# ScalarE's copies of a projection put in front of tile 0's block, in the layers of 8 heads

## The chip, the cores and the metric

The kernel runs on one core of one Trainium2 chip. A core has TensorE (matrix products, PE in the profile), VectorE (DVE), ScalarE (ACT), GpSimd (POOL) and SyncE (SP, which here only starts DMA transfers). Each engine works through its own stream of instructions in order; engines wait for each other by semaphores. The metric is device time in microseconds (us), the median of several executions. All arithmetic of the layers is in float32.

## The reference

Two graph attention layers of 8 heads and one of a single head over 4096 nodes of 512 features. The adjacency matrix is dense int32, but only about 0.2% of it is ones, with more in the first rows and columns. The heart of each layer, cut to what matters:

```python
h = jnp.einsum('nf,kfp->knp', node_matrix, W)          # projection, 8 heads of 64
f1 = jnp.einsum('knp,kp->kn', h, a_src)
f2 = jnp.einsum('knp,kp->kn', h, a_dst)
e = jax.nn.leaky_relu(f2[:, :, None] + f1[:, None, :], negative_slope=ALPHA)
e = jnp.where(adjacency_matrix[None, :, :] > 0, e, NEG_INF)
att = jax.nn.softmax(e, axis=-1)
out = jnp.einsum('knm,kmp->knp', att, h)
...
x = _layernorm(x + _L0_gnn_ref(...))                   # layer 0
h = jax.nn.elu(_gat_heads(x, mask, W1, a1))            # layer 1, 8 heads
h2 = _gat_heads(x1, mask, Wo[None], ao[None])[0]       # layer 2, 1 head of 512
out = jax.nn.relu(elu(h2) @ lin1_w + lin1_b) @ lin2_w + lin2_b
return _layernorm(x + out)
```

## The kernel before

The nodes are cut into 32 tiles of 128. The kernel first finds the edges of tiles 1 to 31 and lists them, while it projects the input for layer 0 (0 to about 325 us of the profile). Then come the two layers of 8 heads (`heads_layer`, L1679: about 325 to 850 us, and 850 to 1305 us), and then the layer of one head with the two linear layers and the last norm.

A layer of 8 heads reads a table in DRAM with one row for each node: 8 heads of 64 projected features, each with the node's score. Tiles 1 to 31 gather the rows of their edges from that table (GpSimd's indirect DMA, L1350), in units of at most six chunks of 128 edges. A unit's steps are: scores and two exponentials (`at.weights`, VectorE and ScalarE, L1442 to L1456), scaling of the gathered rows (`at.scale`, VectorE, L1507 and L1526) and the sums (`at.sum`, TensorE, L1548). Tile 0 has so many edges that it is done densely, by the class `First`: all 32 blocks of 128 rows of the table are loaded by SyncE (`ask`, L1592), `make` turns a block's scores into weights on ScalarE (L1607 to L1612, 18 instructions), `sort_out` masks them on VectorE (L1620), and `add` sums two blocks at a time on TensorE (L1634).

When a tile is finished it goes straight on to the projection of the next layer, over a list of jobs called `ways`, each of which names the job that follows it:

- `divide`: division by the sum of weights and, in layer 0, the residual and the norm, in layer 1 the elu (VectorE, ScalarE L1656 and L1657, or L1667 and L1668)
- `norm`: the rest of that, then `turn_in`: four transposes on TensorE into `pt` (L714) and copies to `xt` on ScalarE (L717)
- `project`: eight matmuls on TensorE into two halves `ph` (L726)
- `rows`: `project_out`, ScalarE's copies of the halves to `hrow` (L753, and L749 where the next layer has one head) and of the scores to `ss_t` (L760), and the store of `hrow` to the next table by SyncE (L754)
- `row`, `split`: rows of tile 0's scores, and scores split into bfloat16 parts

`pt` and `ph` share two PSUM buffers (tag "ph", pool `ps`), so a transpose that follows a projection needs the copies of the projection's first half to be done. `xt` and `hrow` have two buffers each.

The loop of `heads_layer` has one step for each unit and is a manual schedule: each engine gets its instructions in the order of the Python text. In most of the layer the steps come in threes: a tile with few edges (one unit), then a tile with many (two units). The second step of the tile with many edges runs `project`, `make`, `rows` and the transposes of `norm`; the step after it runs `project`, `make`, `First.add` and `rows`; the third runs the transposes of `norm` only. The job list lets a job run one step after the job before it, save that `rows` follows `project` within the step.

Of the kernel before, what the change touches and what calls it, by code (L numbers as in the profile page):

```python
# [560 lines left out]
def sparse_path(  # L561
# [148 lines left out]
    def turn_in(sb, ps, st, src, t):  # L710

        pt = ps.tile([P, FC, P], F32, name="pt", tag="ph")
        for c in range(FC):
            nc.tensor.transpose(pt[:, c, :], src[:, ts(c, P)], ident)  # L714
        xt = sb.tile([P, FC, P], F32, name="xt")
        for c in range(FC):
            nc.scalar.activation(  # L717
                xt[:, c, :], pt[:, c, :], AF.Copy, accum_out=st.xparts[:, c, t : t + 1]
            )
        return xt  # L720
# [8 lines left out]
    def project_in(ps, st, columns, n=P):  # L729

        return [project_half(ps, st, columns, j, n) for j in range(2)]
# [46 lines left out]
    def row_of_s(diag, ps, st):  # L778

        per = min(st.heads, 4)  # L780
        for lo in range(0, st.heads, per):
            for h in range(per):
                nc.scalar.activation(diag[:, lo + h], ident, AF.Copy, scale=st.s[:, 0, lo + h : lo + h + 1])
            pr = ps.tile([P, 4, P], F32, name="pr", tag="ph")[:, :per]
            nc.tensor.matmul(pr, ones_w, diag[:, lo : lo + per], start=True, stop=True)
            nc.scalar.copy(st.s_row[:, lo : lo + per], pr)
# [525 lines left out]
    def units_of(order):  # L1312
        units = []
        for t in order:
            if t == 0:
                steps = math.ceil(NT / GC)
                cuts = [NT * i // steps for i in range(steps + 1)]
                units += [Whole(a, b) for a, b in zip(cuts, cuts[1:])]
                continue
            own = [  # L1320
                Unit(t, [(p.first + i, n) for i, n in runs], slots)
                for p in pts if p.t == t for runs, *slots in p.units()
            ]
            own[0].first = own[-1].last = True
            units += own
        return units
# [352 lines left out]
    def heads_layer(gp, wk, sb, pp, st, nxt, fetch, finish, clear):  # L1679

        many = [t for i in range(8) for t in (2 + i, NT // 2 - i)][: NT // 2 - 1]
        order = [t for pair in zip(range(NT - 1, NT // 2, -1), many) for t in pair] + [1]
        assert sorted(order) == list(range(1, NT))
        units = units_of(order)
        units[-1:] = units[-1].cut(units[-1].n - 2)
        units[:1] = units[0].cut(2)
        groups = [(1, 1), (2, 6), (8, 8), (16, 8), (24, 8)]  # L1690
        with tc.tile_pool(name=f"ha_{st.name}", bufs=2, space=PSUM, reuse_waits="tile") as pacc, \
                tc.tile_pool(name=f"hp_{st.name}", bufs=1, space=PSUM, reuse_waits="tile") as one, \
                tc.tile_pool(name=f"hq_{st.name}", bufs=2, space=PSUM, reuse_waits="tile") as ps, \
                tc.manual_schedule():
            at = Attention(st, gp, wk, pacc, one, whole)
            extra = {}
            if clear:
                for _ in range(GB):
                    nc.vector.memset(gp().rearrange("p k f -> p (k f)").bitcast(BF16), 0.0)
            first = First(at, whole, pacc, order[:-1] + [0, 1])  # L1700
            first.ask()
            for u in units[:GB]:
                at.gather(u)
            for t in order[:2]:
                extra[t] = fetch(t)
            for _ in range(DW):
                first.make()
                first.sort_out()
            first.add(DW)
            first.take()  # L1710
            for t in order[:2]:
                at.spread(t)()
            at.weights(units[0])

            def divide_first():
                at.inverse(sb, 0)
                o = at.normal(sb, 0, spare())
                finish(o, 0, extra.pop(0))()  # L1720
                return norm, 0, o, lambda: None

            def spare():
                return first.sb.tile([P, F + HS], F32, name="rows0", bufs=DW)[:, :F]

            def divide(t):
                at.inverse(sb, t)
                o = at.normal(sb, t)
                return norm, t, o, finish(o, t, extra.pop(t))

            def norm(t, o, rest):
                rest()
                xt = turn_in(pp, ps, nxt, o, t)
                return project, t, xt

            def project(t, xt):
                return rows, t, project_in(ps, nxt, lambda c: xt[:, c, :])

            def rows(t, halves):
                project_out(pp, nxt, halves, t)  # L1740
                out_.add(t)
                if t == 0:
                    return row, 0
                lo, n = next((lo, n) for lo, n in groups if lo <= t < lo + n)
                return (split, lo, n) if out_.issuperset(range(lo, lo + n)) else None

            def row(t):
                row_of_s(first.sb.tile([P, HS, P], F32, name="w0", bufs=DW), ps, nxt)

            def split(lo, n):  # L1750
                split_s(pp, nxt, lo, n)

            def run(of):

                mine = [way for way in ways if way[0] is of]
                for way in ([w for w in mine if w[1] != 0] or mine)[:1]:
                    ways.remove(way)
                    nxt_ = of(*way[1:])
                    if nxt_:
                        ways.append(nxt_)  # L1760

            ways, out_, resting = [], set(), None
            for i, u in enumerate(units):
                pos = order.index(u.t)
                spread = None
                if u.first and pos + 2 < NT - 1:
                    spread = at.spread(order[pos + 2])
                    extra[order[pos + 2]] = fetch(order[pos + 2])
                run(project)
                if i + 1 < len(units):  # L1770
                    at.weights(units[i + 1])
                taken = u.first and first.sorted - first.summed >= min(DB, NT - first.summed) > 0
                if i > 0:
                    first.make(i)
                held = None
                at.scale(u)
                first.take()
                if taken:
                    first.add(DB)
                    held = divide(order[pos - 1]) if pos > 0 else None  # L1780
                    if first.summed == NT:
                        extra[0] = fetch(0, spare())
                        resting = i + 2
                at.sum(u)
                if i + GB < len(units):
                    at.gather(units[i + GB])
                late_split = [way for way in ways if way[0] is split]
                run(rows)
                run(row)
                if first.sorted < first.made - 1 or first.made == NT:  # L1790
                    first.sort_out()
                run(norm)
                if held:
                    ways.append(held)
                elif u.first and pos > 0:
                    ways.append((divide, order[pos - 1]))
                    run(divide)
                if i == resting:
                    ways.append(divide_first())
                if spread:  # L1800
                    spread()
                if late_split:
                    run(split)
            assert resting and resting < len(units) - 4
            assert all(way[0] is split for way in ways)
            ways.append((divide, order[-1]))
            run(divide)
            mrow = mean_of_all_but(pp, ps, nxt, order[-1])
            while ways:
                for of in (project, rows, row, split, norm, divide):  # L1810
                    run(of)
                    if of is rows and len(out_) == NT:
                        finish_mean(ps, nxt, mrow)
# [99 lines left out]
    def gp():  # L1913

        turns[0] += 1
        return (keep if (turns[0] - 1) % GB < GT else more).tile([P, GC, F + HS], F32, name="g")
# [415 lines left out]
```

## Time and profile before

| what | value |
|---|---|
| median of 3 runs | 2067.4 us (2067.35 to 2068.75) |
| the profiled execution's own time | 2044.31 us |
| its span in the profile | 2042.5 us |
| PE / DVE / ACT / POOL busy over the span | 81% / 67% / 44% / 49% |
| PE, DVE, ACT busy in 325 to 850 us (layer 0) | 401.68, 400.91, 260.72 of 525.00 us |
| PE, DVE, ACT busy in 850 to 1305 us (layer 1) | 359.55, 307.34, 241.13 of 455.00 us |
| mean granted TensorE clock over the span | 0.912 of full speed |

In a line of the timeline stand the start, the duration, the engine, the line of the kernel, the operation and what it writes and reads, and in brackets how long the engine had stood idle before it and who ended that wait. "remote" or "another core or an unknown queue" means that the profile names no releaser; "issue" that it shows nothing that was waited for. In a list of waits the three numbers are the total, the number of times and the longest. A busy TensorE is not TensorE at its peak: the ends of matmuls are modelled.

### The profile page before, as it was taken

The page shows a single profiled execution, that of the slowest core. Times are in us where ns is not written, and L with a number is a line of the kernel's source. Part 1 is how long each engine was busy: PE and PEld are TensorE (multiplying, and loading weights), DVE is VectorE, ACT ScalarE, POOL GpSimd, SP SyncE. Part 2 cuts the span into 40 slices and gives each one's busy share as a digit, 9 for nine tenths or more (in the row PEclk, how much of TensorE's full clock was granted, in tenths as well). Part 3 has the DMA queues.
Part 4 walks back from the last instruction along what each step waited for, and adds up shares of the span by engine and source line. Part 5 has one row for each costly group of instructions (what it writes and reads, how often), then busy time and mean ns, then how long its engine had stood idle before and what let it go on. Part 6 is the DMA issues. An engine that isn't in the chain of part 4 may idle for free.

```text
span 2042.5 us, 31094 instructions
## 1 busy us (share of the span) xinstructions
PE 1660.7 (81%) x9797; PEld 1225.7 (60%) x9797; DVE 1360.8 (67%) x3539; ACT 905.5 (44%) x3292; POOL 1000.6 (49%) x1336
## 2 busy tenths in 40 slices
PE   4997975788788878588778787768899998989987
PEld 1675654466556655356556665446668776766776
DVE  6786764888877878377667675426665666656665
ACT  5986964555544636166556562212133221212211
POOL 5556565656654562566655455263432544435100
PEclk7998986888888999789999898878899999999998
DMA  8898855566666664556655555263345444445210
GB/s 309 293 340 285 310 198 165 174 196 195 196 187 188 190 202 132 158 162 175 179 152 150 145 154 166 92 210 112 92 150 164 137 127 125 117 126 139 63 42 33
DMA packets 140084, 343.69 MB, mean 168 GB/s; under 512 B 39525, under 2 KB 44653, under 8 KB 132230
## 3 DMA queue, kind: packets, MB, share of 16 engines
q0 software_dynamic: 64064, 180.85, 31.8%
q1 hardware_dynamic: 74246, 156.57, 22.1%
q10 hardware_dynamic: 1600, 4.19, 0.6%
q8 instruction: 80, 1.31, 0.3%
q14 instruction: 94, 0.77, 0.1%
HBM read 332.19 MB, written 42.24 MB: 183 GB/s over the span
## 4 chain that ended last, share of the span: by engine, by line
PE 46%; issue 12%; ACT 11%; DVE 11%; POOL 5%; another core or an unknown queue 3%; DMA 2%; ACTq 0%; POOLq 0%; DVEq 0%; SPq 0%
PE acc L1548 13%; PE ph L726 11%; PE acc L1634 5%; POOL g L1350 4%; ACT w L1610 3%; PE px L2059 3%; ACT rows L1612 2%; DMA g<-table_t,idx 2%; PE px L2067 2%; PE pt L714 2%; PE py L2059 2%; PE pz L2059 2%; ACT xt L717 1%; PE py L2067 1%
## 5 line engine op out<-in xcount | busy, mean ns | idle before, releaser
L1350 POOL DMA_INDIRECT g<-table_t,idx x774 | 816.3, 1055 | 733.1 <-PE acc L1548 317.6
L1548 PE MATMUL acc<-g,sm 128*64 128x260 f32 (+2 forms) x3408 | 474.8, 411 | 120.2 <-DVE sm L1515 53.1
L726 PE MATMUL ph<-sw_t,xt 128*128 128x264 f32 (+1 forms) x1536 | 408.4, 422 | 78.6 <-issue 35.6
L1548 PEld LDWEIGHTS acc<-g,sm 128*64 128x64 f32 x3408 | 270.7, 145 | 286.8 <-issue 79.6
L726 PEld LDWEIGHTS ph<-sw_t,xt 128*128 128x128 f32 x1536 | 313.4, 209 | 153.1 <-issue 42.4
L1526 DVE TENSOR_TENSOR g<-g,wp 128x2048 f32<-128x2048 f32 (+5 forms) x114 | 291.8, 2559 | 2.8 <-ACT wp L1456 2.8
L717 ACT ACTIVATE xt<-pt 128x128 f32<-128x128 f32 x256 | 67.3, 277 | 253.2 <-PE pt L714 207.2
L1610 ACT ACTIVATE w<-s_row,d 128x128 f32<-128x128 f32 x512 | 155.8, 386 | 0.0
L1634 PE MATMUL acc<-rows,w 128*128 128x65 f32 x1024 | 125.4, 283 | 18.9 <-DVE w L1620 18.7
L1634 PEld LDWEIGHTS acc<-rows,w 128*128 128x128 f32 x1024 | 125.3, 201 | 21.7 <-ACT rows L1608 19.2
L1158 DVE MAX8 cand<-key 128x8 f32<-128x85 f32 (+51 forms) x395 | 99.7, 316 | 45.0 <-PE key L992 44.9
L1612 ACT ACTIVATE rows<-rows 128x64 f32<-128x64 f32 x512 | 128.6, 334 | 0.0
L977 ACT ACTIVATE sg<-raw,value 128x2048 bf16<-128x2048 int32 x60 | 120.1, 2008 | 5.1 <-DMA raw<-in_adj_dram 4.7
L2073 ACT ACTIVATE shid<-shid,sl1b 128x256 f32<-128x256 f32 x112 | 50.5, 500 | 119.3 <-DVE shid L2011 111.6
L714 PE MATMUL pt<-s_ident,o 128*128 128x128 f32 x248 | 42.8, 298 | 56.9 <-ACT ss_t L760 34.6
L1667 ACT ACTIVATE rstd<-mv,s_eps 128x1 f32<-128x1 f32 x64 | 18.9, 295 | 140.7 <-DVE mv L1664 132.0
L1658 DVE SCALAR_TENSOR_TENSOR o<-ex,o 128x512 f32<-128x512 f32 x63 | 43.6, 691 | 53.2 <-ACT ex L1657 43.6
L1620 DVE SCALAR_TENSOR_TENSOR w<-w,mask 128x1024 f32<-128x1024 f32 x64 | 77.3, 1211 | 1.2 <-ACT w L1610 1.2
L714 PEld LDWEIGHTS pt<-s_ident,o 128*128 128x128 f32 x248 | 27.6, 146 | 83.0 <-ACT ss_t L760 40.1
L1555 DVE RECIPROCAL rd_t<-acc 128x8 f32<-128x8 f32 x62 | 12.7, 204 | 94.0 <-PE acc L1548 39.9
L1656 ACT ACTIVATE ex<-o 128x512 f32<-128x512 f32 x63 | 39.6, 629 | 77.2 <-DVE o L1574 55.0
L1515 DVE TENSOR_SCALAR sm<-iota_n,nl,w 128x64 f32<-128x64 f32 x284 | 68.4, 317 | 0.0
(283 smaller groups left out, 2839.6 us busy)
## 6 DMA issues: line engine op xcount, KB each, us to landing
raw<-in_adj_dram SPq DMA_DIRECT2D x60, 1024.0 KB
table_t<-hrow SPq DMA_DIRECT2D x64, 260.0 KB
rows<-table_t SPq DMA_DIRECT2D x64, 260.0 KB
xr<-in_x_dram SPq DMA_DIRECT2D x63, 256.0 KB
g<-table_t,idx POOLq DMA_INDIRECT x774
table_t<-hrow SPq DMA_DIRECT2D x32, 257.0 KB
xr<-sx_d SPq DMA_DIRECT2D x32, 256.0 KB
out_dram<-xr SPq DMA_DIRECT2D x32, 256.0 KB
```

Source lines behind the costliest of these rows:

```text
L714: nc.tensor.transpose(pt[:, c, :], src[:, ts(c, P)], ident)
L717: nc.scalar.activation(xt[:, c, :], pt[:, c, :], AF.Copy, accum_out=st.xparts[:, c, t : t + 1])
L726: nc.tensor.matmul(ph[:n], columns(c), st.w[:, c, j], start=(c == 0), stop=(c == FC - 1))
L977: nc.scalar.activation(sg[:, ts(i, w)], raw[:, ts(i, w)], AF.Sign, bias=values["half"])
L1158: nc.vector.max(out=cand[:, at : at + 8], in_=key[:, j - w0_ : j - w0_ + n_])
L1350: nc.gpsimd.indirect_dma_start(out=u.g[:, k, : self.st.row], out_offset=None, in_=self.st.table[:, :], in_offset=bass.IndirectOffsetOnAxis ...
L1526: nc.vector.tensor_mul(body, body, wp[:, :, None].to_broadcast(body.shape))
L1548: nc.tensor.matmul(out_[g * HN : (g + 1) * HN], sm[:, slot], rows(k), start=start, stop=stop)
L1610: nc.scalar.activation(w[:, h], self.st.s_row[:, h], AF.Exp, scale=0.8, bias=d8[:, h : h + 1])
L1612: nc.scalar.activation(rows[:, h, :DM], rows[:, h, :DM], AF.Copy, scale=rows[:, h, DM : DM + 1])
L1634: nc.tensor.matmul(acc[:, j, k * HD : (k + 1) * HD], w[:, h], rows[:, h * HD : (h + 1) * HD], start=(b == lo and k == 0), stop=(b == hi - ...
L2059: nc.tensor.matmul(out_[:, m], a[:, c, ts(k, P)], b[:, c], start=m == 0 and c == 0, stop=k == ks[-1] and c == 1,)
```

## The change

Two statements of the step move up: the list of `split` jobs that stood before this step's `rows`, and `run(rows)` itself. They stood behind `at.sum` and the gathers; now they stand in front of `first.make(i)`. No statement is added or removed.

```diff
@@ -1770,6 +1770,8 @@
                 if i + 1 < len(units):
                     at.weights(units[i + 1])
                 taken = u.first and first.sorted - first.summed >= min(DB, NT - first.summed) > 0
+                late_split = [way for way in ways if way[0] is split]
+                run(rows)
                 if i > 0:
                     first.make(i)
                 held = None
@@ -1784,8 +1786,6 @@
                 at.sum(u)
                 if i + GB < len(units):
                     at.gather(units[i + GB])
-                late_split = [way for way in ways if way[0] is split]
-                run(rows)
                 run(row)
                 if first.sorted < first.made - 1 or first.made == NT:
                     first.sort_out()
```

On ScalarE the copies L749, L753 and L760 of a step now stand ahead of the block L1607 to L1612 of the same step, and in layer 0 or 1 ahead of what `divide` issues within `held`. On SyncE the store L754 stands ahead of the loads L1592 and L1922 of the same step. The order on TensorE, VectorE and GpSimd is the same in both kernels.

## The prediction

> **What bounds the kernel now.** I read the page first, then the chain of waits through the two layers of 8 heads (325 to 1240 us), then the sum of waits there, then single steps in the timeline.
>
> From the page: the shares of the chain, and the groups concerned.
>
> ```profile
> PE 46%; issue 12%; ACT 11%; DVE 11%; POOL 5%; another core or an unknown queue 3%; DMA 2%; ACTq 0%; POOLq 0%; DVEq 0%; SPq 0%
> ...
> L1610 ACT ACTIVATE w<-s_row,d 128x128 f32<-128x128 f32 x512 | 155.8, 386 | 0.0
> ...
> L1612 ACT ACTIVATE rows<-rows 128x64 f32<-128x64 f32 x512 | 128.6, 334 | 0.0
> ```
>
> TensorE is the largest link, but ScalarE has 11%, and of it L1610 and L1612, the block of tile 0 that `make` issues, are the largest lines. The waits of 325 to 1240 us (total us, times, longest):
>
> ```profile
> ACT xt L717 <- remote: 39.5, 9, 8.0
> ...
> PE pt L714 <- ACT ss_t L760: 34.6, 12, 4.5
> ...
> ACT hrow L753 <- remote: 15.6, 9, 2.5
> ```
>
> TensorE's transposes wait for the small copies of L760 that `rows` makes. With the L753 and L749 waits of the same kind that is 54.7 us before L714 in this stretch. The timeline shows one such step of layer 1:
>
> ```profile
> 923.24 3.74 PE L726 MATMUL ph<-sw_t,xt 128*128 128x257 f32 x16 [0.76 <-issue]
> ...
> 925.35 0.16 ACT L1607 ACTIVATE d<-rows 128x8 f32<-128x8 f32 x1
> ...
> 926.90 1.97 PE L1548 MATMUL acc<-g,sm 128*64 128x260 f32 x16
> ...
> 928.00 2.00 ACT L1612 ACTIVATE rows<-rows 128x64 f32<-128x64 f32 x8
> ...
> 930.52 0.16 ACT L760 COPY ss_t<-ph 128x1 f32<-128x1 f32 x1
> ...
> 930.68 0.66 PE L714 MATMUL pt<-s_ident,o 128*128 128x128 f32 x4 [1.80 <-ACT ss_t L760]
> ...
> 931.37 0.28 ACT L717 ACTIVATE xt<-pt 128x128 f32<-128x128 f32 x1 [0.69 <-issue]
> ```
>
> The projection ends at 926.98, yet its copies start after the block, so the transposes stand 1.80 us. The round goes ScalarE's xt copies, projection, block, copies, transposes, xt copies. Of every three steps one has this round (call it the tight step): it projects, makes a block and transposes. The step before it makes no block, and the one after it transposes nothing. I count 11 tight steps in layer 0 and 11 in layer 1. Elsewhere ScalarE waits 4 to 10 us for the transposes and has room.
>
> **What the Trainium skill says.** "Perfetto Trace Analysis", section "Per-instruction lifecycle": ScalarE and VectorE are strict first in, first out. The trace agrees: the copies above, ready at 926.98, wait behind the block until 929.99. The same section: a matmul's end is computed, its semaphore comes later. The trace agrees strongly; at 1122.26 the sums of a tile end by the record, and who needs them starts at 1129.20:
>
> ```profile
> 1124.07 0.66 PE L714 MATMUL pt<-s_ident,o 128*128 128x128 f32 x4 [1.80 <-ACT hrow L749]
> ...
> 1129.20 0.21 DVE L1555 RECIPROCAL rd_t<-acc 128x8 f32<-128x8 f32 x1 [4.75 <-remote]
> ...
> 1132.04 0.28 ACT L717 ACTIVATE xt<-pt 128x128 f32<-128x128 f32 x1 [7.97 <-remote]
> ```
>
> "TensorE: Matmul & The Clock Gate", section "Part 1: The HAM clock gate": an idle window of about 3.4 us halves the clock. Here the granted clock falls to 0.50 in 1128 to 1132, and the projection after the tight step takes 5.2 to 6.6 us instead of 3.74 in some 17 of 22 cases.
>
> **The change, part by part.** It removes and adds no instruction. VectorE's, TensorE's and GpSimd's orders stay. On ScalarE the 4 or 5 copies of `rows` go in front of the 18 instructions of the block. On SyncE 15 table stores go ahead of the loads of tile 0's rows (L1592). POOL's queue is not passed.
>
> *The tight step.* Let P be the start of its projection and E the time at which ScalarE is done with the exponentials. Now: block 4.69 us (925.35 to 930.00 and alike), copies 0.74, transposes and hand-over 0.69; xt starts at E + 6.12. After: the copies must wait for the projection. What that gives is seen in a step that makes no block, at 774.20:
>
> ```profile
> 774.20 3.83 PE L726 MATMUL ph<-sw_t,xt 128*128 128x264 f32 x16 [0.46 <-issue]
> ...
> 778.07 0.38 ACT L753 COPY hrow<-ph 128x260 f32<-128x260 f32 x1 [1.40 <-PE ph L726]
> 778.34 0.23 ACT L760 COPY ss_t<-ph 128x4 f32<-128x4 f32 x2
> ```
>
> The second copy starts at P + 3.87, all are done at P + 4.43 (in layer 1, with one small copy less, P + 4.25). Then the block, then xt at once, for the transposes now lie beside the block. So xt starts at 4.69 after the later of E + 0.74 and P + 4.43. The block stays in the round: only the transposes leave it, and the wait for the projection enters.
> - Layer 0: E is P + 3.6 on average (2.4 to 4.8; L1456 writes the one `wp` buffer and stands up to 3.5 us before it). Over the 11 steps the differences are -0.69 to +0.57 us, sum -4.3 us.
> - Layer 1: E is P + 2.1. Before P + 8.13, after P + 8.94: +0.8 us in ten steps, 0 in one (E = P + 2.9). Sum +8.1 us.
> - Together +4 us. The 54.7 us before L714 are thus hardly to be had: the same ScalarE time is waited for by L717's reader, the next projection, instead.
>
> *Late hand-overs.* In the 22 steps xt starts later than E + 6.12 by 45.5 us in all, which the page mostly puts to a remote releaser: in order 1.3, 0, 0.6, 0.3, 3.8, 2.3, 3.4, 0.6, 4.7, 0, 0.5 in layer 0 and 3.2, 0, 2.6, 0, 5.2, 2.6, 3.8, 1.7, 7.3, 0, 1.8 in layer 1. After, transposes end near P + 6.4 to 7.3, about 2.2 us before the block ends; taking 2.2 us from each of the 22 excesses leaves 16.8, so 28.7 us gone. Against that the project-to-copy hand-over, now in front of the block, comes into the round. In the 14 steps without a block it was late by 0, 0.85, 2.2, 2.8, 4.0 or 4.7 us, 14.5 in all, 1.04 each; 22 times that is +22.8. Bounds: 0, if it is prompt while TensorE is busy behind it; and above, seven tight steps in which the second copy waited to P + 9 or later even behind the block, where the block would now start only then: 3.8 us each, +27 net. I take the mean, because the steps without a block have just the order that comes. Sum so far: +4 - 28.7 + 22.8 = -2 us.
>
> *The clock.* The stake is about 1.9 us in 17 projections, 32 us. TensorE's gap before the transposes (3.1 us in layer 0, 1.8 in layer 1, then a second one) becomes one gap behind them, shorter by the little that the round gains. Three of 17 back at full clock would be -6 us. Bounds 0 and -15; I take -6.
>
> *The step after it* (projection, block, no transposes): the copies wait for P + 3.9, at half clock P + 6.5, and the block, the layer norm's or elu's instructions and the next exponentials move back by 3 to 5.5 us. Behind them stands the xt copy that idles 4 to 10 us for the transposes: cost 0; without that cover 1 to 2 us in each of the few steps with only 4 us.
>
> *VectorE* waits up to 1.4 us longer for the block at L1620 in that step (930.79 above); behind it stand the next unit's scores and the scaling, needed only after the projection and tile 0's 3.5 us: 0. *SyncE*: a store waits for copies that end before tile 0's sums, for which the loads behind it wait anyway: 0; a late load would be felt only two steps on (REST).
>
> Sum -8 us of the profiled execution's 2044.31 us (span 2042.5). The median shown is 2067.4, 23 us more, so late hand-overs may be commoner there; I carry the difference: 2059.
>
> **The rivals.**
> - *Hand-overs and clock recover.* They come mostly where TensorE stands, and it now has its transposes early. All 45.5 us gone: -41.5 with the +4; 2026. For it: hand-overs behind a busy TensorE are mostly prompt (0 in 8 of 14). Against: TensorE still idles 2.4 us before the projection.
> - *The projection in front of the block*, the slower one. Place: the second copy of `rows` in the tight step. Price: all that it is late beyond E now delays 4.69 us of block and with it xt; decides once the copy is late by more than about 2 us per step on average. With the seven late steps as above and layer 1's +0.8: about +19; 2086. For it: 15.6 us of L753 waits even behind the block. Against: 774.20.
> - *Nothing changes*: the terms cancel within 0.2% (about what a measurement of this kernel tells from no change); 2067.
>
> **How the numbers follow.** Small gain 0.42 (own range 2045 to 2064), recovery 0.12, slower 0.32 (2072 to 2095), nothing 0.14. Faster 0.53, with nearly all of the first case; same 0.15; slower 0.32. The range 2034 to 2088 leaves out most of the recovery and the upper end of the slower case.
>
> **What would show it.** L714's waits for L760, L753 and L749 fall from 54.7 us to under 15. L753's waits for the projection rise from 18 us to over 60. L717 in the tight step starts right behind L1612, without idle, at P + 9. The idle before L726 grows. Wrong, if xt in the tight steps of layer 1 starts before P + 8.5, or if VectorE or PE waits for w at L1620 by more than 20 us, or if L753 in the tight steps waits past P + 6 in more than a third.

## The result, and the profile after

The changed kernel takes 2102.1 us (median of 6 runs, 2088.0 to 2106.4), the kernel before 2066.5 us beside it. The ratio of the runs is 1.0159 (95%: 1.0131 to 1.0186; the medians alone give 1.0172): 1.6% slower, where 0.4% faster had been predicted. The profiled execution took 2087.99 us (span 2086.3), 43.7 us more than that of before.

From the page of the changed kernel: the shares of the chain, and two of the costliest groups.

```profile
PE 47%; issue 11%; DVE 11%; ACT 11%; another core or an unknown queue 5%; POOL 4%; DMA 3%; POOLq 0%; DVEq 0%; ACTq 0%; SPq 0%
...
L726 PE MATMUL ph<-sw_t,xt 128*128 128x264 f32 (+1 forms) x1536 | 423.5, 434 | 126.2 <-ACT xt L717 61.6
...
L753 ACT COPY hrow<-ph 128x260 f32<-128x260 f32 (+2 forms) x128 | 47.8, 374 | 219.5 <-PE ph L726 146.6
```

Over the whole program ScalarE now idles 219.5 us ahead of the copies of L753. The share of the chain that has no releaser in the record rose from 3% to 5%. The waits of 325 to 1280 us (total us, times, longest):

```profile
ACT hrow L753 <- PE ph L726: 132.3, 71, 4.6
ACT xt L717 <- PE pt L714: 109.8, 30, 6.8
PE ph L726 <- ACT xt L717: 60.2, 34, 7.9
ACT hrow L753 <- remote: 57.5, 18, 5.9
...
DVE o L1658 <- ACT ex L1657: 22.7, 12, 2.4
...
DVE rstd L1672 <- ACT rstd L1668: 18.1, 12, 4.3
...
PE pt L714 <- ACT ss_t L760: 10.9, 4, 4.5
```

Two waits of the kernel before (325 to 1240 us) that belong beside these:

```profile
PE ph L726 <- ACT xt L717: 33.5, 23, 7.6
...
ACT hrow L753 <- PE ph L726: 18.2, 14, 2.4
```

The wait that the change was to remove is mostly gone: L714 waits for `rows`' copies 10.9 us instead of 54.7. In its place ScalarE waits in front of L753 for the projection, 132.3 and 57.5 us where it was 18.2 and 15.6, and the projection waits more for xt (60.2, before 33.5). VectorE's waits at L1658 and L1672 are new: in the kernel before they are 0 and 3.4 us.

One tight step of layer 0 in the timeline (start, us, engine, line; idle before it and its releaser in brackets):

```profile
402.65 3.83 PE L726 MATMUL ph<-sw_t,xt 128*128 128x264 f32 x16 [0.46 <-ACT xt L717]
...
406.75 1.97 PE L1548 MATMUL acc<-g,sm 128*64 128x260 f32 x16 [0.28 <-issue]
407.04 0.38 ACT L753 COPY hrow<-ph 128x260 f32<-128x260 f32 x1
412.76 0.38 ACT L753 COPY hrow<-ph 128x260 f32<-128x260 f32 x1 [5.34 <-remote]
...
413.25 0.68 PE L714 MATMUL pt<-s_ident,o 128*128 128x128 f32 x4 [4.52 <-ACT ss_t L760]
...
415.86 2.00 ACT L1612 ACTIVATE rows<-rows 128x64 f32<-128x64 f32 x8
417.77 0.25 ACT L717 ACTIVATE xt<-pt 128x128 f32<-128x128 f32 x1
...
418.17 1.25 PE L726 MATMUL ph<-sw_t,xt 128*128 128x264 f32 x2 [4.00 <-issue]
```

By the record the projection is done at 406.48, yet its second copy starts at 412.76, P + 10.1. The block follows it, xt follows the block at once, and the next projection starts after 4 us of idle, at half speed (6.69 us for all of it at a granted clock of 0.50, where the one before took 3.83 at 1.00). This is the picture of the slower rival.

I cut both traces at the first xt copy of every transposing step. The last xt copy of layer 1 comes 46 us later than before. Of these, the 22 tight steps have 14.8 us (252.0 to 266.8), the 22 steps after them 7.8 (358.9 to 366.7), the four intervals around the last blocks of the two layers 7.9 (56.8 to 64.7), the start of layer 1 5.5 (55.4 to 60.9), everything else about 10. Not all of this is the change's doing. The profiled execution of before was a quick one (2044 us, where the median is 2067), and a second profile of before (before_again, below) has 61.5 us at the start of layer 1 and 61.1 around the last blocks. A second profile of the changed kernel was taken on the same chip as that one, both near their medians. Between these two the last xt copy comes 24.2 us later: 16.9 from the tight steps (252.5 to 269.4), 4.6 from the steps after them (361.6 to 366.2), 2.6 from around the last blocks, and the rest about nothing. So the tight steps carry most of the loss.

### The profile page after: what moved, and what is told of

Read it like the earlier page. It is cut to its first block, busy times and chain, and to the rows that moved or that the text cites. A ratio compares the mean times of both kernels' runs of the same rounds, so it can differ in the third digit from the quotient of the medians.

```text
span 2086.3 us, 31062 instructions
## 1 busy us (share of the span) xinstructions
PE 1669.0 (80%) x9777; PEld 1232.9 (59%) x9797; DVE 1363.4 (65%) x3539; ACT 912.4 (44%) x3292; POOL 999.0 (48%) x1336
## 4 chain that ended last, share of the span: by engine, by line
PE 47%; issue 11%; DVE 11%; ACT 11%; another core or an unknown queue 5%; POOL 4%; DMA 3%; POOLq 0%; DVEq 0%; ACTq 0%; SPq 0%
PE ph L726 15%; PE acc L1548 13%; PE acc L1634 4%; ACT w L1610 3%; POOL g L1350 3%; PE px L2059 3%; ACT rows L1612 2%; PE py L2059 2%; DMA g<-table_t,idx 2%; PE px L2067 2%; PE pz L2059 2%; DVE g L1526 1%; DVE xr L2011 1%; PE acc L1478 1%
## 5 line engine op out<-in xcount | busy, mean ns | idle before, releaser
L726 PE MATMUL ph<-sw_t,xt 128*128 128x264 f32 (+1 forms) x1536 | 423.5, 434 | 126.2 <-ACT xt L717 61.6
L726 PEld LDWEIGHTS ph<-sw_t,xt 128*128 128x128 f32 x1536 | 323.6, 216 | 206.5 <-ACT xt L717 68.8
L1610 ACT ACTIVATE w<-s_row,d 128x128 f32<-128x128 f32 x512 | 155.8, 386 | 0.0
L753 ACT COPY hrow<-ph 128x260 f32<-128x260 f32 (+2 forms) x128 | 47.8, 374 | 219.5 <-PE ph L726 146.6
L717 ACT ACTIVATE xt<-pt 128x128 f32<-128x128 f32 x256 | 66.6, 272 | 142.8 <-PE pt L714 119.0
L1612 ACT ACTIVATE rows<-rows 128x64 f32<-128x64 f32 x512 | 128.5, 334 | 0.0
L1658 DVE SCALAR_TENSOR_TENSOR o<-ex,o 128x512 f32<-128x512 f32 x63 | 43.5, 690 | 79.5 <-ACT ex L1657 75.3
L1620 DVE SCALAR_TENSOR_TENSOR w<-w,mask 128x1024 f32<-128x1024 f32 x64 | 77.6, 1215 | 5.4 <-ACT w L1610 4.6
L1648 DVE TENSOR_TENSOR total<-total,acc 128x520 f32<-128x520 f32 x28 | 19.5, 695 | 83.0 <-PE acc L1634 77.7
L1656 ACT ACTIVATE ex<-o 128x512 f32<-128x512 f32 x63 | 39.6, 629 | 72.1 <-DVE o L1574 54.1
L2067 PE MATMUL px<-sl2w,shid 128*128 128x256 f32 x256 | 63.1, 390 | 0.0
```

Of the source, the lines that this page charges most:

```text
L726: nc.tensor.matmul(ph[:n], columns(c), st.w[:, c, j], start=(c == 0), stop=(c == FC - 1))
L1610: nc.scalar.activation(w[:, h], self.st.s_row[:, h], AF.Exp, scale=0.8, bias=d8[:, h : h + 1])
L1612: nc.scalar.activation(rows[:, h, :DM], rows[:, h, :DM], AF.Copy, scale=rows[:, h, DM : DM + 1])
L1620: nc.vector.scalar_tensor_tensor(w, w, 1.0, mask0[:, self.turns[b], None, :].to_broadcast([P, HS, P]), op0=OP.max, op1=OP.mult)
L2067: nc.tensor.matmul(out_[:, :HF], a[:, k, ts(r, P)], b[:, k], start=k == 0, stop=k == 3)
```

## The experiments

Sixteen runs were made in four sets, each set on one chip beside the kernel before. Before took 1934.8 us in the first set, and 2063.5, 2068.2 and 2052.5 us in the others. That 6 to 7% goes with the chip, and it turned out to be the key. (Whether it is the chip itself, or the condition in which it ran at the time, one set on each chip cannot tell.) "Prompt chip" below is that of the first set, "late chips" are the other three and that of the result. Ratios are to before on the same chip.

**The change cut in two.** Copies ahead of the block only in the second unit of a tile (all tight steps), and only in the first unit (the steps after them):

```diff
+                ahead = not u.first          # light_ahead: ahead = u.first
+                late_split = [way for way in ways if way[0] is split]
+                if ahead:
+                    run(rows)
                 if i > 0:
                     first.make(i)
...
-                late_split = [way for way in ways if way[0] is split]
-                run(rows)
+                if not ahead:
+                    run(rows)
```

> The copies stand in front of the block only in the units that are not the first of their tile (the tight steps, which also transpose, and three steps at the start of a layer); everywhere else as before. Theory A (the block and with it the xt copies wait for the late projection copy in the tight steps): this kernel has most of the loss, 25 to 35 us over before. Theory B (both kinds of step pay: in the light steps elu, exponentials and, at the end of a layer, a second block stand behind the late copy): 12 to 20 us over before, as the times from one xt to the next in the two traces differ by 15 us in the tight steps. Theory C (the order of SyncE's stores and loads): about half the steps, about half the loss, with no longer time from xt to xt in the tight steps.

> The reverse: the copies stand in front of the block only in the first unit of a tile (the light steps that divide and do not transpose, and the last two steps with a block at the end of each layer). Theory A: at most 10 us over before. Theory B: 15 to 24 us over before, of which some 8 us where the layer's last two blocks follow each other, and VectorE's waits at L1658 and L1672 of about 20 us each. Theory C: about half the loss without those waits.

Measured on the prompt chip: heavy_ahead 0.9996 (0.9982 to 1.0010), light_ahead 1.0072 (1.0053 to 1.0091), +14 us. For theory A that is a miss: with the copies ahead of the block in the tight steps the kernel is as fast as before there. A tight step of heavy_ahead:

```profile
896.99 3.74 PE L726 MATMUL ph<-sw_t,xt 128*128 128x257 f32 x16 [0.46 <-ACT xt L717]
...
900.77 0.38 ACT L753 COPY hrow<-ph 128x257 f32<-128x257 f32 x1 [1.26 <-PE ph L726]
...
902.57 0.66 PE L714 MATMUL pt<-s_ident,o 128*128 128x128 f32 x4
...
903.81 2.00 ACT L1612 ACTIVATE rows<-rows 128x64 f32<-128x64 f32 x8
905.72 0.25 ACT L717 ACTIVATE xt<-pt 128x128 f32<-128x128 f32 x1
```

The second copy starts at P + 3.78 and xt at P + 8.7, right behind the block: the prediction's model to 0.2 us. No wait for L753 or L717 in that trace is put to a remote releaser. In light_ahead, where the loss is, the waits of 320 to 1240 us are:

```profile
ACT hrow L753 <- PE ph L726: 97.0, 63, 3.0
...
DVE o L1658 <- ACT ex L1657: 26.8, 13, 6.7
...
DVE rstd L1672 <- ACT rstd L1668: 14.9, 11, 2.2
```

The steps after the tight ones are 4.8 us longer in sum than in heavy_ahead, and the intervals around the last blocks 4.6 us. There VectorE stands at elu and the layer norm for ScalarE, which stands for the projection. Another 7.8 us lie in the tight steps, which in light_ahead have the order of before. As no profile of before was taken on the prompt chip, how the 14 us divide among these three places is not shown.

The same two kernels on a late chip:

> heavy_ahead once more, for a chip on which completions reach ScalarE late (before at about 2063 us instead of 1935). There, theory A: the loss of the change is made in the tight steps, where the block now waits for a late projection copy: 15 to 25 us over before, tight steps 15 us longer in sum than before's 252. Theory B: at most 8 us over before. If the chip is again one with prompt completions: 0, as before.

> light_ahead once more. Chip with late completions: theory A: the rest of the change's 32 us, 5 to 15 us, and since light_mid is 3 us faster than before there, all of it in the last two steps with a block in each layer. Theory B: 25 us or more. Chip with prompt completions: +14 us again.

heavy_ahead_2: 1.0212 (1.0188 to 1.0235), +42 us, the tight steps 287.7 us in sum. light_ahead_2: 1.0018 (1.0001 to 1.0035), +3 us. Here theory A holds, more strongly than expected: the whole loss is made where the copies stand ahead of the block in the tight steps. The second copy starts at P + 7.29 on average, against P + 4.01 for the same program on the prompt chip. A late one, of the same shape as the prompt step above:

```profile
1057.35 3.73 PE L726 MATMUL ph<-sw_t,xt 128*128 128x257 f32 x16 [0.46 <-ACT xt L717]
...
1066.11 0.37 ACT L753 COPY hrow<-ph 128x257 f32<-128x257 f32 x1 [6.24 <-remote]
...
1071.05 0.26 ACT L717 ACTIVATE xt<-pt 128x128 f32<-128x128 f32 x1
```

The copy starts at P + 8.76 and xt at P + 13.7, again right behind the block.

**The kernels themselves again**, for profiles beside the others:

> The kernel before itself, for a profile on the same chip as the other runs of this set: same time as before within 0.3%. Where completions reach ScalarE at once (as in the four runs above, whose before took 1934.8 us), its tight steps take 10.5 us (layer 0) and 8.5 us (layer 1) from xt to xt, and no wait is put to a remote releaser. Rival: the late hand-overs (36.7 us at L717 in the first profile) belong to the kernel and are there again.

> The changed kernel on the same chip. If the parts add up and completions are prompt here: heavy_ahead (0) plus light_ahead (+14 us) gives 10 to 18 us over before, that is 0.5 to 0.9%, with tight steps of 9.3 us in layer 0 and 9.1 us in layer 1. If the loss of 35 us (1.6%) does not depend on late hand-overs: 28 to 40 us over before here too.

> The changed kernel beside its two halves. Chip with late completions: +28 to +40 us, the sum of the two halves. Chip with prompt completions: +10 to +18 us, all of it from the light half, with tight steps of 9.3 us in layer 0 and 9.1 us in layer 1.

Both sets fell on late chips. before_again: 1.0001, with 45.6 us of remote waits at L717 in 325 to 1280 us, so the late hand-overs are there again; that they belong to the kernel alone is excluded by the prompt chip. The changed kernel: 1.0157 (1.0117 to 1.0197) and 1.0144 (1.0104 to 1.0185), second copy at P + 6.23 and P + 6.08. That it is less slow than heavy_ahead_2 means that the parts don't add up. With the copies ahead in the other steps as well, both kinds of step are shorter: after_3, on the same chip as heavy_ahead_2, has 270.7 us in the tight steps and 368.2 in the steps after them, against 287.7 and 374.2. The profile of heavy_ahead_2 is of the slowest of its six runs, 10 us above their median, so part of that difference is chance; why the rest is gained is open. The whole change was not run on the prompt chip.

**The end of the layers.** light_ahead with `ahead = u.first and first.made < NT - 2`, that is without the last two steps with a block:

> light_ahead without the last two steps with a block in each layer: the copies stand in front of the block only in the 11 or so light steps of each layer. If the end of the layers (two blocks behind one another, both behind late copies) costs what the traces show, 4 to 8 us of light_ahead's 14 go, leaving 6 to 10 us over before. Rival (all of the loss is in the regular light steps, which VectorE's waits at L1658 and L1672 carry): 12 us or more remain.

It fell on a late chip: 0.9984 (0.9965 to 1.0002), no change, and less than both forecasts. Against light_ahead_2 on another late chip the intervals around the last blocks fall from 67.6 to 57.1 us; before_again, on the chip of light_mid, has 61.1, so profiles differ there by some 4 us without any change of the kernel. In the changed kernel the one of layer 1 looks like this:

```profile
1240.15 0.37 ACT L753 COPY hrow<-ph 128x257 f32<-128x257 f32 x1 [2.53 <-remote]
...
1243.31 1.22 DVE L1620 SCALAR_TENSOR_TENSOR w<-w,mask 128x1024 f32<-128x1024 f32 x1 [2.31 <-ACT w L1610]
...
1246.40 0.69 DVE L1658 SCALAR_TENSOR_TENSOR o<-ex,o 128x512 f32<-128x512 f32 x1 [1.87 <-ACT ex L1657]
...
1247.15 1.11 PE L714 MATMUL pt<-s_ident,o 128*128 128x128 f32 x4 [3.25 <-DVE o L1658]
...
1251.11 0.26 ACT L717 ACTIVATE xt<-pt 128x128 f32<-128x128 f32 x1
```

Two blocks follow each other here, so the first one's delay reaches elu, the transposes, the second block and xt. This is where the cover that the prediction named, ScalarE's idle time before xt, is missing.

**Copies inside the block**, behind L1610 and ahead of L1612:

```diff
+        def make(self, step=0, between=lambda: None):
...
             for h in range(HS):
                 nc.scalar.activation(w[:, h], self.st.s_row[:, h], AF.Exp, ...)
+            between()
             for h in range(HS):
                 nc.scalar.activation(rows[:, h, :DM], rows[:, h, :DM], AF.Copy, ...)
...
-                    first.make(i)
+                    first.make(i, lambda: run(rows))
```

> The copies stand inside the block: behind the exponentials of L1610 and in front of the products of L1612. ScalarE then has 2.7 us of the block to do before it needs the projection. Theory A: the copies wait 30 us or less for the projection, the transposes lie beside L1612, xt starts at E + 5.4 instead of E + 6.1 or later in the tight steps, and the kernel is 0 to 20 us faster than before, 2047 to 2067. Rival (the transposes' early start is what hurts, or the order on SyncE, both of which this kernel shares with the change): slower than before by over 20 us like the change.

> between (the copies between the block's exponentials and its products) once more. Chip with late completions: the copies come at P + 4.8 to P + 6.3, so a hand-over that is late by 2.7 us on average costs about 1 us in a tight step instead of 2.7; xt at P + 9.3 instead of P + 10.8 to P + 11.3; 15 to 35 us faster than before. Rival (late completions move to the next hand-over and nothing is gained): within 8 us of before. Chip with prompt completions: 27 us faster again.

Prompt chip 0.9859 (0.9844 to 0.9873), 27 us faster; late chip 1.0080 (1.0055 to 1.0106), 14 us slower, a miss. On the late chip the second copy starts at P + 8.14 and the products still come behind it. The order that is right on one chip is wrong on the other.

**Only the first half ahead.** `rows` is cut in two: the first half's copies ahead of the block, the second's at their old place.

```diff
                 return half0, t, project_in(ps, nxt, lambda c: xt[:, c, :])
+            def half0(t, halves):
+                hrow = pp.tile([P, F + HS], F32, name="hrow")[:, : nxt.row]
...
+                part_out(nxt, hrow, halves[0], 0, t)
+                return rows, t, halves, hrow
...
+            def rows(t, halves, hrow):
+                part_out(nxt, hrow, halves[1], 1, t)
+                nc.sync.dma_start(nxt.table[ts(t, P), :], hrow)
...
+                run(half0)
                 if i > 0:
                     first.make(i)
```

> Only the copies of the projection's first half (and its piece of ss_t) stand in front of the block; those of the second half, whose hand-over is the late one, stay behind it. The transposes need only the first half's buffer, so they lie beside the block, and xt starts at E + 5.4 (block 4.69, copies 0.74) without the transposes' 0.69. Theory A (what costs in the change is the second copy's late hand-over, because it stands in front of the block): none of the loss is left; chip with late completions: 15 to 40 us faster than before, chip with prompt ones: 8 to 20 us faster. Rival D (completions come late whatever is queued, and a late second copy behind the block delays xt just as much): within 10 us of before.

0.9996 (0.9982 to 1.0010) on a late chip. The loss is gone, so what half_ahead left at its old place carries it: the second half's copy, or the store to the table on SyncE, which stayed behind the block with it. The traces settle which. If the store held up SyncE's loads, the block would wait for its rows at L1607; that wait is 2.2 us in the changed kernel and 2.5 in heavy_ahead_2, against 2.1 in before_again (325 to 1280 us). So it is the second half's copy. But there is no gain either, so rival D holds for that part. half_ahead was not run on the prompt chip. A tight step:

```profile
401.31 3.83 PE L726 MATMUL ph<-sw_t,xt 128*128 128x264 f32 x16 [0.60 <-issue]
...
406.69 0.38 ACT L738 COPY hrow<-ph 128x260 f32<-128x260 f32 x1 [1.34 <-PE ph L726]
...
407.48 0.63 PE L714 MATMUL pt<-s_ident,o 128*128 128x128 f32 x4 [0.35 <-issue]
...
409.73 2.00 ACT L1612 ACTIVATE rows<-rows 128x64 f32<-128x64 f32 x8
411.63 0.35 ACT L738 COPY hrow<-ph 128x260 f32<-128x260 f32 x1
...
411.94 0.27 ACT L717 ACTIVATE xt<-pt 128x128 f32<-128x128 f32 x1
```

The transposes stand 0.35 us and lie beside the block, and the second copy finds its data ready behind it. Taking the transposes' wait away altogether was worth next to nothing on such a chip: the tight steps take 250.2 us in sum, in the two profiles of before 252.0 and 252.5.

**Does TensorE's standing make the completions late?** The changed kernel, with each half's `ss_t` copy directly behind its `hrow` copy, so that the transposes need the first half only:

> The changed kernel, but each half's ss_t copy follows its own hrow copy, so the transposes no longer wait for the second half; TensorE goes on to them without standing. Theory H1 (completions come late because TensorE stands idle behind the sums, and it stands because it waits for those very copies): the second copy falls from P + 6.2 to about P + 4.5 in the tight steps and the loss of 32 us on a chip with late completions shrinks to 10 us or less. Theory H2 (they come late whatever TensorE does next): the second copy stays at P + 6 and the loss at 25 to 35 us. On a chip with prompt completions the kernel stands as the change does, 10 to 18 us over before.

1.0080 (1.0052 to 1.0108) on a late chip, half the loss. The transposes start at P + 6.3 instead of P + 7.2, the second copy at P + 5.82, not at P + 4.5. The waits of 320 to 1190 us are hardly smaller:

```profile
ACT hrow L753 <- PE ph L726: 102.1, 55, 5.8
...
ACT hrow L753 <- remote: 44.9, 13, 7.4
```

A tight step:

```profile
461.48 3.83 PE L726 MATMUL ph<-sw_t,xt 128*128 128x264 f32 x16 [1.32 <-ACT xt L717]
...
467.16 0.64 PE L714 MATMUL pt<-s_ident,o 128*128 128x128 f32 x4
...
470.42 0.38 ACT L753 COPY hrow<-ph 128x260 f32<-128x260 f32 x1 [3.86 <-remote]
```

TensorE goes on to the transposes at P + 5.68 without standing, and yet the second copy starts at P + 8.94. So the wait of the transposes is not what makes the completion late, and H1's two figures both miss. That TensorE's idling has no part in it is not shown: by the record it stands again behind the transposes and the small products that follow them, from 467.93. H2 missed the size of the loss; the copy is 0.26 to 0.41 us earlier than in the three profiles of the change, times 22 that is 6 to 9 us, about what the tight steps are shorter (259.7 against 266.8 to 270.7, on other chips). The rest of the saving is not accounted for.

**The block out of the round.** No block in the tight steps; it is made one step earlier:

```diff
-REST = 2
+REST = 1
...
+                tight = {rows, norm} <= {way[0] for way in ways}
-                if i > 0:
+                if i > 0 and not tight:
                     first.make(i)
```

> Order of before, but no block in the tight steps: it is made one step earlier, in the step that has no projection's copies and in which ScalarE waits 4 to 10 us for the transposes (REST 1 instead of 2). If the block in the round xt, projection, block, copies, transposes, xt is what sets the tight steps (the prediction's view of before), they lose up to 4 us each and the kernel is 40 to 80 us faster than before, less what the next step hands back. Rival (the round is set by the projection and what VectorE and TensorE do behind it, so the block is hidden): within 10 us of before.

> No block in the tight steps, once more. Chip with late completions: the tight steps lose the block but keep the late copies, 20 to 40 us; the light steps hand some of it back, as in third_between, which is 8 us faster than before; 0 to 25 us faster than before. Chip with prompt completions: 34 us faster again.

> Both edits that gained: no block in the tight steps (made one step earlier), and in the light steps the copies between the exponentials and the products of the block. third gained 34 us of which the tight steps are 40; between gained 27. If what between gains lies in the tight steps (its xt to xt there is 23 us shorter than in light_ahead), the two do not add up: 30 to 40 us faster than before. If it lies in the light steps (15 us shorter there than in heavy_ahead): 45 to 60 us faster.

> half_ahead and third in one: no block in the tight steps, first halves ahead of the block in the light ones. If the two gains lie in different steps they add up, 30 us or more faster than before on either kind of chip; if the tight steps are then bound by the late completion of the projection alone, it is as third_2 within 8 us.

third: 0.9820 (0.9804 to 0.9837) on the prompt chip, 34 us faster and the best there. third_2 0.9952 (0.9929 to 0.9975) and third_half 0.9945 (0.9924 to 0.9967) on a late chip, third_between 0.9971 (0.9954 to 0.9988) on another. third is the one kernel that was run on both kinds of chip and was faster than before on both; its gain on the late chip is a quarter of that on the prompt one, and with the other edits on top (third_between, third_half, run on late chips only) it gained no more. Waits of third_2 (320 to 1260 us):

```profile
ACT hrow L753 <- remote: 55.2, 14, 6.4
ACT d L1607 <- DMA rows<-table_t: 53.7, 24, 4.8
```

Without a block to hide it the late copy (P + 7.7) is in the round itself: the tight steps fall from 252 to 226.4 us only, on the prompt chip they take 169.7. And the earlier blocks wait for their rows from SyncE.

## Why the prediction was wrong, step by step

- *The tight step without lateness (+4 us: -4.3 in layer 0, +8.1 in layer 1)*: right in the sign of both layers, and in the single step to 0.2 us, but not in the sum. On the prompt chip, heavy_ahead against light_ahead (block first), the tight steps differ by -11.2 us (106.5 against 117.7) and +3.4 us (100.6 against 97.2), together -7.8. The two kernels differ in the other steps too, so this is a comparison, not a measurement of the term alone.
- *Late hand-overs (-28.7 + 22.8 us)*: this is the step that failed, and it decides the sign. Of its two halves the first held: of the 45.5 us by which xt was late, 16.8 were to remain, and ScalarE's idle time before xt in the tight steps is 11.5, 12.8 and 16.9 us in the three profiles of the change. The second was half of what came: the project-to-copy lateness, taken as 1.04 us a step from 14 steps without a block, is 2.2 us in the tight steps (P + 6.16 against P + 4.01), 47 us in sum and not 22.8. With these two figures the prediction's own sum for the tight steps is +4 - 34 + 47 = +17 us; measured are 14.8 in the result's two profiles and 16.9 in the two of one chip. Taking the prompt chip's sums as the floor says the same: beyond it the tight steps take 37 us in before (252.0 less light_ahead's 214.9) and 60 us after (266.8 less heavy_ahead's 207.1), where a fall from 45.5 to 39.6 was predicted. Those 14 steps stand at the ends of the layers and were no sample of the tight ones. The prediction had the sign in its hands: it counted seven tight steps with a copy past P + 9 even behind the block, and set the mean of the other steps against them.
- *What was called lateness of the transposes* was not theirs to lose. In before, the block lay over the late completion of the projection; moving the copies ahead of it took that cover away. half_ahead shows it: same early transposes, late half behind the block, no loss.
- *The clock (-6 us)*: wrong in sign. The projections after the tight steps that take over 4.5 us are 17 and 19 of 22 in the two profiles of before, and 22, 22 and 21 in the three of the change. In sum these 22 projections take 117.7 and 119.7 us in before and 125.5 to 126.2 in the change, 6 to 8 us more. The two gaps of before became one, with a late xt behind it: in the step shown 4.00 us.
- *The step after it (0)*: right on a late chip for the regular steps (light_mid 0.9984): the 5 to 8 us by which they grow in the change are about what their slower projections take more. Wrong for the last blocks of the layers, by 2.6 to 7.9 us in the two pairs of profiles, and wrong on the prompt chip (light_ahead +14 us), where it is not shown how much of it lies in these steps. The cover is not free: xt there waits for transposes that themselves wait for ScalarE's elu or norm behind the block.
- *VectorE and SyncE (0)*: the mask at L1620 is not late by much (4.6 us in all), as said. But L1658 and L1672, 22.7 and 18.1 us, were not on the list of those who wait. SyncE's order was not tried by itself, but the block's wait for its rows did not grow (2.1 us in before_again, 2.2 in the change), and no other wait for a load of SyncE grew either.
- *The rivals*: the slower one, with its place and mechanism, is what happened. Its point of decision, late by more than about 2 us on average, is where the run stands (2.2 us). Its price is another matter: +19 does not follow from the terms that it names, for 27 from the seven late steps and 4 for the tight step give 31. The tight steps measure 14.8 to 16.9, the slower projections behind them 6 to 8. Of the signs named, L714's fall under 15, L753's rise over 60 and xt right behind L1612 (in 15 of 22 tight steps) came true, and so did the counter-sign: the copy is past P + 6 in 11 of 22 tight steps.

## What to carry to other kernels

Where completions come late, an instruction that waits for one stands better behind work that needs nothing: on the late chips the block in front of the copies was no obstacle but a cover. On the prompt chip there was little to cover, and moving the copies ahead cost nothing in the tight steps (heavy_ahead 0.9996) or even gained (between 0.9859); an order found best on one chip is to be tried on a second. Before such a cover is moved, take the lateness from the very steps that lose it, also from those where it hides behind the cover, and not from calmer ones. And a stall of the bounding engine is only worth what the next wait in the same round leaves of it: here L714's wait for the copies went nearly or wholly in the change, in after_by_half and in half_ahead, and none of them was faster for it on the late chips.

## What the runs showed of the hardware

One program, two speeds: before takes 1934.8 us on one chip and 2052.5 to 2068.2 us on three others, and in the tight steps, where it was looked for, the difference is in completions of TensorE. heavy_ahead, the same program on both: ScalarE's second copy starts at P + 4.01 and at P + 7.29, VectorE's next reciprocal of a tile's sums at P + 10.7 and at P + 13.0 on average; VectorE stands for it in 4 and in 18 of the 22 steps; and no wait at L753 or L717 is put to a remote releaser on the one chip, 72 us of them on the other (325 to 1280 us). The first xt copy comes at 377 and 383 us, the last of layer 1 at 1205 and 1374 us, so 163 of the 185 us by which the spans differ arise in between, in the two layers of 8 heads. TensorE's own record doesn't show it. Stretches of the late step above, in the changed kernel (length, then busy time of PE, PEld, DVE, ACT and POOL, granted clock, DMA share, GB/s):

```profile
402.60:404.60 2.00, 1.95 (x9) 1.69 (x10) 1.86 (x8) 1.23 (x8) 1.62 (x2) 1.00 0.89 246
404.60:406.60 2.00, 1.88 (x9) 1.27 (x7) 2.00 (x4) 0.27 (x1) 1.47 (x2) 1.00 0.99 353
406.60:408.70 2.10, 1.95 (x16) 1.06 (x16) 1.99 (x6) 0.58 (x2) 1.79 (x2) 1.00 0.71 234
408.70:410.70 2.00, 0.03 (x2) 0.00 (x0) 1.93 (x9) 0.00 (x0) 1.39 (x3) 1.00 0.08 21
410.70:413.20 2.50, 0.00 (x0) 0.00 (x0) 2.45 (x3) 0.44 (x4) 0.66 (x2) 1.00 0.63 164
```

By the record the granted clock is 1.00 throughout and TensorE is idle from 408.7, yet the copy starts at 412.76. What delays these completions stays open; after_by_half excludes only that the transposes' wait for the second half does. As the ends of matmuls in the record are modelled, it cannot say whether TensorE was still at work or only its signal late.
